# The last convolution on two row halves of PE, kept pieces of x and early loads, in a two-layer image kernel

## The chip, the cores and the metric

The kernel runs on one core of one Trainium2 chip. The metric is device time in microseconds: the median of three runs. Beside it stands one execution under the hardware profiler, from which every duration below comes. The engines are named as in the profile: PE (TensorE, matmuls), PEld (its weight loads), DVE (VectorE), ACT (ScalarE), POOL (GpSimd) and SP (SyncE, which here only issues DMAs).

## What is computed

The input x is float32 of shape 4 x 192 x 128 x 128. Two residual layers follow each other, each on a group-normalised input (32 groups of 6 channels):

```python
x = x + L0_conv(gn(x))     # layer 0
x = x + L1_conv(gn(x))     # layer 1: layer norm, projections, a depthwise convolution, a selective scan, a gate
```

Only layer 0 is touched by the change. Cut to its steps, with `C1 = 48` and `C0 = 16`:

```python
x1 = c1x1(x, conv1_w)                            # 192 -> 48 channels
x_0, x_05, x_1 = x1[:, :16], x1[:, 16:32], x1[:, 32:48]
Fre = frft2d(x_05, 0.5)                          # fractional Fourier transform, both axes
mag, pha = abs(Fre), angle(Fre)
mag_out = c1x1(c3x3(mag * mask1) * mask1 + c1x1(mag * mask2) * mask2)
pha_out = c1x1(pha)
ifrft = abs(frft2d(polar(mag_out, pha_out), -0.5))
fre = rfft2(x_1); mo, po = c1x1(abs(fre)), c1x1(angle(fre))
x_1o = irfft2(polar(mo, po))
x_0o = c1x1(x_0)
return c1x1(concat([x_0o, ifrft, x_1o]), conv2_w)   # 48 -> 192 channels
```

## The kernel before

Layer 0 handles one image after the other. An image of 192 x 16384 values is cut into 16 pieces of 1024 columns (`NPIECE`, `PIECE`); a piece of x is a tile `xt` of 96 partitions x 2 x 1024 values, 768 KB, since the 192 channels stand as two halves of 96 (index `t`). Three generators do the work:

- `analysis(b)` (L247) reads the 16 pieces for the group statistics (`bn`, four `bn_stats` a piece, L192), works out the group's mean and scale in `bn_done` (L196), and reads the 16 pieces again for the first convolution (L278), whose output goes to DRAM as `d1` (48 rows). This convolution already puts the two column halves `q` of a piece on the two column halves of PE: weights `w1r[:, t, half]`, output partitions 0 to 63 and 64 to 127.
- `branches(b)` (L291) does the transforms of the image: `spectrum` forward (matmuls L214 and L224, then `_polar` on DVE, ACT and POOL), the convolutions on magnitude and phase (L244, L348), `_from_polar`, and the inverse transforms (L407, L415, then L437, L445). Its output `dimg` (32 rows) is written to DRAM at L453. It yields 26 times.
- `synthesis(b)` (L456) does the last convolution and the residual. For each piece it loads x once more (L461), loads a tile `cat` of 49 rows (16 rows of `d1`, 32 of `dimg`, one row of ones `orow` for the bias), multiplies it with the folded weights `w2x` (49 x 192, L471), adds the result to `xt` (L475), takes the statistics for layer 1 (L476), and stores the sum to `xmid` with a DMA from POOL (L477).

For each half `q` of 512 columns, a tile `pr` of two PSUM banks takes the two output halves `t`; both matmuls stand on PE's first rows:

```python
pr = psB.tile([128, 2, 512], F32, name="pr")
for t in range(2):
    nc.tensor.matmul(pr[0:CH, t, :], w2x[:, t * CH : (t + 1) * CH], cat[:, at], start=True, stop=True)
nc.vector.tensor_add(xt[:, :, at], xt[:, :, at], pr[0:CH])
```

A float32 matmul runs as two passes, each with its own weight load: the profile counts 512 of them at L471 for 64 pieces x 4 matmuls.

The generators are interleaved by the loop at the end of `layer0` (L489): at each of the 26 steps of `branches(b)`, `analysis(b + 1)` goes one step, and then either `analysis(b + 1)` (odd steps) or `synthesis(b - 1)` (even steps) goes one more. What is left of both is run after the last step. The last image has no `analysis` beside it, so `synthesis(2)` gets its 13 even steps there and three pieces afterwards; `synthesis(3)` follows alone.

The order on the engines is not the program's order word for word: outside of layer 1 (whose order is written by hand) a scheduler puts instructions in the order of its own plan, and inserts the waits. The program's order is its priority. Each engine then runs its list in that order. Loads, `cat` loads and the transfers of the branches all stand in one queue, SP's; a DMA that has to wait for its buffer holds up what is behind it.

Buffers that matter: `xt` has 6 (pool `l0x`), `cat` 2, `pr` 2 (pool `l0r`, shared with `spectrum`), `ps` 4. A piece's `xt` becomes free when its last reader is done, in `synthesis` when its store has landed.

Layer 1 begins when `bn_done` of the last image is through, because its constants `nmr` (L554) need the statistics of all images.

Of the kernel before, what the change touches and what calls it, by code (L numbers as in the profile page):

```python
# [10 lines left out]
F32 = mybir.dt.float32  # L11
# [8 lines left out]
C = 192  # L20
CH = 96
GROUP = 6
NC = 16
# [9 lines left out]
PIECE = ROWS * S  # L33
NPIECE = S // ROWS
# [87 lines left out]
def layer0(tc, x, xmid, st2, w):  # L122

    nc = tc.nc
    B = x.shape[0]
    with ExitStack() as ctx:
        def pool(name, bufs, **kw):
            return ctx.enter_context(tc.tile_pool(name=name, bufs=bufs, **kw))

        cp = pool("l0c", 1)  # L130
        dram = pool("l0d", 2, space=DRAM)
        xp = pool("l0x", 6)
        sp = pool("l0s", 2)
        imp = pool("l0i", 2)
        zp = pool("l0z", 2)
# [1 line left out]
        qp = pool("l0q", 1)  # L137
# [3 lines left out]
        def const(name):  # L141
            src = w[name]
            t = cp.tile(list(src.shape), F32, name="c_" + name)
            nc.sync.dma_start(out=t, in_=src)
            return t
# [3 lines left out]
        ri_cat, ri_out = const("ri_cat"), const("ri_out")  # L149


        w2x = cp.tile([3 * NC + 1, C], F32, name="w2x")
        nc.sync.dma_start(out=w2x[NC : 3 * NC, :], in_=w["w2T"][NC:, :])
        w20, c0 = cp.tile([NC, C], F32, name="w20"), const("c0")
        nc.sync.dma_start(out=w20, in_=w["w2T"][0:NC, :])
        ps = psA.tile([128, 512], F32, name="ps")
        nc.tensor.matmul(ps[0 : NC + 1, 0:C], c0, w20, start=True, stop=True)
        folded = cp.tile([NC + 1, C], F32, name="folded")
        nc.vector.tensor_copy(folded, ps[0 : NC + 1, 0:C])
        nc.sync.dma_start(out=w2x[0:NC, :], in_=folded[0:NC, :])  # L160
        nc.sync.dma_start(out=w2x[3 * NC :, :], in_=folded[NC:, :])
        half_pi = cp.tile([128, 1], F32, name="half_pi")
        nc.vector.memset(half_pi, math.pi / 2)

# [4 lines left out]
        dmag = []  # L169
        zrow = cp.tile([1, S], F32, name="zrow")  # L170
        nc.vector.memset(zrow, 0.0)
        orow = cp.tile([1, PIECE], F32, name="orow")
        nc.vector.memset(orow, 1.0)
        for i in range(min(2, B)):
            d = dram.tile([NC * S + 2, S], F32, name=f"dmag{i}", bufs=1)
            nc.sync.dma_start(out=d[0:1, :], in_=zrow)
# [3 lines left out]
        def split(v):  # L180
            return v.rearrange("(t p) f -> p t f", p=CH)

        def load(b, p):
            xt = xp.tile([CH, 2, PIECE], F32, name="xt")
            src = x[b].rearrange("c h w -> c (h w)")[:, p * PIECE : (p + 1) * PIECE]
            nc.sync.dma_start(out=xt, in_=split(src))
            return xt

        def bn(st, p, xt):
            for t in range(2):  # L190
                for q in range(PIECE // 512):
                    nc.vector.bn_stats(  # L192
                        st[:, t, p * (PIECE // 512) + q, :], xt[:, t, q * 512 : (q + 1) * 512]
                    )

        def bn_done(st, out):  # L196
            mv = sp.tile([CH, 2, 2], F32, name="mv")
            for t in range(2):
                nc.vector.bn_aggr(mv[:, t, :], st[:, t, :, :])
            _group_stats(nc, sp, psA, g_ones, mv, out, 1e-5)  # L200
# [46 lines left out]
        def analysis(b, got):  # L247


            st = sp.tile([CH, 2, NPIECE * (PIECE // 512), 6], F32, name="st")  # L250
            for p in range(NPIECE):
                bn(st, p, load(b, p))
                yield
            gst = sp.tile([CH, 2, 2], F32, name="gst")
            bn_done(st, gst)

            w1r = sp.tile([CH, 2, 128], F32, name="w1r")
            for t in range(2):  # L260
                nc.vector.tensor_scalar(w1r[:, t, :], w1T[:, t, :], gst[:, t, 1:2], None, ALU.mult)
            ps = psA.tile([128, 512], F32, name="ps")
            for t in range(2):
                nc.tensor.matmul(
                    ps[:, 0:1], w1r[:, t, :], gst[:, t, 0:1], start=t == 0, stop=t == 1
                )
            b1 = sp.tile([128, 1], F32, name="b1")
            nc.vector.tensor_scalar(b1, ps[:, 0:1], -1.0, None, ALU.mult)
            d1 = got["d1"] = dram.tile([3 * NC, S * S], F32, name="d1")
            for p in range(NPIECE):  # L270
                xt = load(b, p)
                if p % 2 == 0:
                    x1 = sp.tile([128, 2, 512], F32, name="x1")
                ps = psA.tile([128, 512], F32, name="ps")
                for t in range(2):
                    for q in range(2):
                        half = slice(64 * q, 64 * (q + 1))
                        nc.tensor.matmul(  # L278
                            ps[half], w1r[:, t, half], xt[:, t, q * 512 : (q + 1) * 512],
                            start=t == 0, stop=t == 1,  # L280
                        )
                nc.scalar.activation(x1[:, p % 2, :], ps, AF.Identity, bias=b1)
                if p % 2 == 1:
                    at = d1[:, (p - 1) * PIECE : (p + 1) * PIECE].rearrange(
                        "c (e q f) -> q c e f", e=2, q=2
                    )
                    for q in range(2):
                        nc.scalar.dma_start(out=at[q], in_=x1[64 * q : 64 * q + 3 * NC])
                yield
# [163 lines left out]
            nc.sync.dma_start(out=dimg.rearrange("c h w -> h c w"), in_=img)  # L453
            got.update(dimg=dimg)

        def synthesis(b, got):  # L456

            d1, dimg = got["d1"], got["dimg"].rearrange("c h w -> c (h w)")
            st = sp.tile([CH, 2, NPIECE * (PIECE // 512), 6], F32, name="st2")
            for p in range(NPIECE):  # L460
                xt = load(b, p)  # L461
                cat = qp.tile([3 * NC + 1, PIECE], F32, name="cat", bufs=2)
                at = slice(p * PIECE, (p + 1) * PIECE)
                nc.sync.dma_start(out=cat[0:NC, :], in_=d1[0:NC, at])
                nc.sync.dma_start(out=cat[NC : 3 * NC, :], in_=dimg[:, at])
                nc.sync.dma_start(out=cat[3 * NC :, :], in_=orow)
                for q in range(PIECE // 512):
                    at = slice(q * 512, (q + 1) * 512)
                    pr = psB.tile([128, 2, 512], F32, name="pr")
                    for t in range(2):  # L470
                        nc.tensor.matmul(  # L471
                            pr[0:CH, t, :], w2x[:, t * CH : (t + 1) * CH], cat[:, at],
                            start=True, stop=True,
                        )
                    nc.vector.tensor_add(xt[:, :, at], xt[:, :, at], pr[0:CH])  # L475
                bn(st, p, xt)  # L476
                nc.gpsimd.dma_start(  # L477
                    out=split(xmid[b][:, p * PIECE : (p + 1) * PIECE]), in_=xt
                )
                yield  # L480
            bn_done(st, st2[:, b])

        got = [{} for _ in range(B)]
        for _ in analysis(0, got[0]):
            pass
        behind = iter(())
        for b in range(B):  # L489
            ahead = analysis(b + 1, got[b + 1]) if b + 1 < B else iter(())  # L490
            for i, _ in enumerate(branches(b, got[b])):
                next(ahead, None)
                next(ahead if i % 2 else behind, None)
            for rest in (behind, ahead):
                for _ in rest:
                    pass
            behind = synthesis(b, got[b])
        for _ in behind:
            pass

# [3 lines left out]
def layer1(tc, xmid, out, st2, w, n_tok=S * S):  # L504

    nc = tc.nc
    B = len(xmid)
    NCHUNK = n_tok // T
# [8 lines left out]
    with ExitStack() as ctx:  # L517
# [35 lines left out]

        nmr = cp.tile([CH, B, 2], F32, name="nmr")  # L554
        nc.vector.scalar_tensor_tensor(
# [600 lines left out]
def program(tc, x, out, w):  # L1156
    B = x.shape[0]
    with (
        tc.tile_pool(name="keep", bufs=1) as keep,
        tc.tile_pool(name="mid", bufs=1, space=DRAM) as mid,  # L1160
    ):
        st2 = keep.tile([CH, B, 2, 2], F32, name="st2")
        xmid = [mid.tile([C, S * S], F32, name=f"xmid{b}") for b in range(B)]
        layer0(tc, x, xmid, st2, w)
        layer1(tc, xmid, [out[b].rearrange("c h w -> c (h w)") for b in range(B)], st2, w)
# [16 lines left out]
```

## Time and profile before

| what | us |
|---|---|
| median of 3 runs (lowest, highest) | 11733.97 (11728.79, 11737.78) |
| the profiled execution, whole | 11752.54 |
| its span, first to last instruction | 11750.5 |
| `dimg` of image 0, 1, 2, 3 issued to DRAM | 401.6, 700.8, 1035.8, 1308.5 |
| first matmul of the last `synthesis` | 1326.35 |
| end of its last statistics | 1438.9 |
| median time to landing: `xt` load, `xmid` store, `dimg` write | 9.4, 7.2, 14.8 |

How to read it: busy times are sums over a stretch, so a share of busy time averages over stages with different limits. What ends a wait is named behind an arrow, by engine, tile and line. In the lists of the timeline the columns are start, duration, engine, line, operation, output and inputs, and how many are merged; in brackets, the idle time before and what ended it. "SPq" and "ACTq" are DMAs issued from those engines. The granted clock is that of PE, as a fraction of full speed.

Over the whole span DVE is busy 92%, POOL 86%, PE 85% and ACT 73%, but that is layer 1's picture, which fills seven eighths of the time. Layer 0 has its own, and differs from stage to stage.

### The profile page before, as it was taken

Reading aid. Unit: us, or ns where it says so; the run is one execution under the profiler, and the core shown is the slowest. Engines: PE = TensorE matmul, PEld = TensorE weight load, DVE = VectorE, ACT = ScalarE, POOL = GpSimd, SP = SyncE. Lnnn points to the kernel's source line nnn. Section 1 sums busy time; section 2 is a strip of 40 time slices with the busy share of each in tenths; the row PEclk is TensorE's granted clock in tenths of the full one; section 3 lists DMA queues with packets and bytes.
Section 4 is the critical chain, followed back from the end, with each engine's and each line's share of the span. In section 5 each row is a group of like instructions: output and inputs, shape, how many; then the busy total and the mean of one; then the engine's idle time right before and its main releaser. Section 6 shows DMA issues by size and latency. Waiting matters only on the chain.

```text
span 11750.5 us, 153548 instructions
## 1 busy us (share of the span) xinstructions
PE 9994.0 (85%) x50570; PEld 6788.1 (58%) x50570; DVE 10759.5 (92%) x11584; ACT 8606.6 (73%) x14436; POOL 10087.8 (86%) x4598
## 2 busy tenths in 40 slices
PE   4777888888888888888888888888888888888887
PEld 2444456666666666666666666666666666666665
DVE  5565579999999999999999999999999999999999
ACT  2322178788888788788788788788888878878876
POOL 0000089999999999999999999999999999999999
PEclk8888689999999999999999999999999999999998
DMA  8887633433433443443443443443343343344343
GB/s 208 209 223 194 185 109 113 124 114 111 124 117 108 124 123 103 126 125 100 126 124 102 123 124 106 120 124 108 117 124 113 113 124 115 111 124 118 108 124 97
DMA packets 1339384, 1494.09 MB, mean 127 GB/s; under 512 B 903473, under 2 KB 954358, under 8 KB 1338070
## 3 DMA queue, kind: packets, MB, share of 16 engines
q1 hardware_dynamic: 1318102, 1421.34, 42.0%
q0 software_dynamic: 13312, 50.34, 1.3%
q10 hardware_dynamic: 7168, 12.59, 0.3%
q8 instruction: 398, 6.52, 0.2%
q14 instruction: 404, 3.31, 0.1%
HBM read 1325.19 MB, written 155.32 MB: 126 GB/s over the span
## 4 chain that ended last, share of the span: by engine, by line
DVE 42%; ACT 20%; PE 19%; issue 12%; DMA 4%; POOL 1%; DVEq 1%; SPq 0%; ACTq 0%; POOLq 0%
DVE h L868 29%; DVE op L819 10%; PE py L894 5%; ACT da L799 5%; ACT op L799 4%; PE ps L663 3%; ACT dbT L843 2%; ACT L799 2%; PE pr L471 2%; PE py L908 2%; ACT dt L744 1%; DMA xt<-in_x 1%; ACT L744 1%; DMA bc<-dbc 1%; PE ps L653 1%
## 5 line engine op out<-in xcount | busy, mean ns | idle before, releaser
L881 POOL TENSOR_TENSOR hc<-h,bc 128x1024 f32<-128x1024 f32 x3072 | 7198.0, 2366 | 244.7 <-DVE h L868 218.7
L868 DVE TENSOR_TENSOR_SCAN h<-da,carry,op 128x512 f32<-128x512 f32 x3968 | 4945.7, 1271 | 2.3 <-issue 0.5
L894 PE MATMUL py<-ident,hc 128*128 128x128 f32 x24576 | 3482.6, 291 | 680.1 <-ACT yt L903 653.5
L894 PEld LDWEIGHTS py<-ident,hc 128*128 128x128 f32 x24576 | 3049.8, 151 | 1585.1 <-issue 754.3
L799 ACT ACTIVATE da<-dt,c_A_log 128x512 f32<-128x512 f32 x4096 | 2813.7, 721 | 558.2 <-DVE h L868 551.9
L868 DVE TENSOR_TENSOR_SCAN h<-op,carry,db 128x512 f32<-128x512 f32 x1984 | 2522.3, 1271 | 84.2 <-issue 82.2
L827 POOL TENSOR_TENSOR db<-dtu,bc 128x1024 f32<-128x1024 f32 x1024 | 2419.6, 2363 | 7.9 <-DMA bc<-dbc 7.8
L819 DVE TENSOR_TENSOR op<-dp,bc 128x512 f32<-128x512 f32 x3328 | 2252.5, 677 | 32.9 <-ACT dp L782 32.9
L799 ACT ACTIVATE op<-dt,c_A_log 128x512 f32<-128x512 f32 x2048 | 1398.8, 689 | 979.0 <-DVE h L868 978.8
L663 PE MATMUL ps<-s,c_wiT 96*128 96x512 f32 x3072 | 1468.5, 601 | 38.4 <-DVE s L657 38.4
L681 PE MATMUL ps<-xs,dcw 128*128 128x512 f32 x3072 | 1424.3, 592 | 0.2 <-ACT xs L676 0.2
L799 ACT ACT_TABLE_LOAD x636 | 816.0, 1283 | 11.5 <-DVE h L868 0.3
L843 ACT ACTIVATE dbT<-ps,bT 128x128 f32<-128x128 f32 x3072 | 822.0, 371 | 0.0
L932 PE MATMUL ps<-yg,c_woT 128*96 128x512 f32 x1536 | 711.8, 599 | 112.6 <-DVE xm L938 112.6
L663 PEld LDWEIGHTS ps<-s,c_wiT 96*128 96x128 f32 x3072 | 531.3, 193 | 445.9 <-issue 376.7
L681 PEld LDWEIGHTS ps<-xs,dcw 128*128 128x128 f32 x3072 | 533.1, 190 | 432.5 <-issue 432.1
L477 POOL DMA_DIRECT2D xmid<-xt x64 | 42.9, 671 | 782.6 <-DVE xt L475 775.9
L908 PE MATMUL py<-ddp,u 128*128 128x128 f32 x3072 | 536.0, 333 | 0.0
L633 PE MATMUL ps<-ones,xs 96*128 96x1 f32 x2048 | 346.2, 299 | 199.0 <-ACT dt L744 194.2
L932 PEld LDWEIGHTS ps<-yg,c_woT 128*96 128x96 f32 x1536 | 240.2, 163 | 472.0 <-issue 318.9
L908 PEld LDWEIGHTS py<-ddp,u 128*128 128x128 f32 x3072 | 511.1, 251 | 0.0
L748 POOL TENSOR_TENSOR dtu<-dt,u 128x512 f32<-128x512 f32 x384 | 476.6, 1269 | 30.1 <-ACT dt L744 30.1
(172 smaller groups left out, 10267.7 us busy)
## 6 DMA issues: line engine op xcount, KB each, us to landing
bc<-dbc SPq DMA_DIRECT2D x1024, 1024.0 KB, 5.9
xt<-in_x SPq DMA_DIRECT2D x192, 768.0 KB, 9.4
xmid<-xt POOLq DMA_DIRECT2D x64, 768.0 KB, 7.2
xm<-xmid SPq DMA_DIRECT2D x128, 384.0 KB, 3.6
carry<-h SPq DMA_DIRECT2D x3072, 1.0 KB, 1.9
out<-xm SPq DMA_DIRECT2D x128, 384.0 KB, 3.3
d<-x ACTq DMA_DIRECT2D x64, 192.0 KB, 7.8
df<-u SPq DMA_DIRECT2D x16, 512.0 KB, 4.9
```

The lines of the kernel that those rows point to most:

```text
L663: nc.tensor.matmul(pp, wiT[:, t, m * 128 : (m + 1) * 128], s[:, t, :], start=t == 0, stop=t == 1)
L681: nc.tensor.matmul(pc, dcw[:, j, k, :], xs[:, j, k : k + T], start=k == 0, stop=k == 3)
L748: nc.gpsimd.tensor_tensor(dtu[j], dt[j], u[j], ALU.mult)
L799: nc.scalar.activation(da, got[n]["dt"][j], AF.Exp, scale=A[:, j, st : st + 1])
L819: nc.vector.tensor_tensor(dbs[s], g["dp"], g["bc", k % NG][:, 0, q, :], ALU.mult)
L827: nc.gpsimd.tensor_tensor(db, _bc(g["dtu"][j], 1, G), g["bc", sg][:, 0], ALU.mult)
L843: nc.scalar.activation(t[:, blk, :], g["tu", j][:, blk, :], AF.Identity, scale=g["bT"][:, blk, q : q + 1])
L868: nc.vector.tensor_tensor_scan(h[:, q, :], das.pop(s), dbs.pop(s) if db is None else db[:, q, :], 0.0 if ch == 0 else g["before"][:, j, st ...
L881: nc.gpsimd.tensor_tensor(hc, h, g["bc", sg][:, 1], ALU.mult)
L894: nc.tensor.matmul(py[:, blk, :], hc[:, q, blk * 128 : (blk + 1) * 128], ident, start=first, stop=sg == NG - 1 and q == G - 1 and blk == T ...
L908: nc.tensor.matmul(got[n]["py", j][:, blk, :], got[n]["u"][j][:, blk * 128 : (blk + 1) * 128], ddp[:, j, :], start=False, stop=False, skip ...
L932: nc.tensor.matmul(po[0:CH], woT[:, j, t * CH : (t + 1) * CH], g["yg", j], start=j == 0, stop=j == NJ - 1,)
```

## The change

The second convolution's tile `cat` becomes two fixed tiles of 128 x 512 values instead of a rotating one of 49 x 1024. Half `q` of a piece is loaded into rows 64q to 64q + 47, and row 64q + 48 holds a one that is written once, at the start; `orow` and its load for each piece go. The weights `w2x` are held twice, on rows 0 to 48 and 64 to 112. A `pr` tile now belongs to one output half `t`, and its two matmuls take the two halves `q`, each from its own rows; the addition runs over all 1024 columns of one `t`.

In `analysis`, the last four pieces of the statistics stay on chip (`KEEP`), and the first convolution begins with them; they aren't read a second time. The pool of `xt` has 7 buffers instead of 6.

For the last image, `synthesis(2)` goes a step at every step of `branches(3)`, and at step 18 (`LOADS`) the first four pieces of x for `synthesis(3)` are loaded (`early`).

```diff
-        xp = pool("l0x", 6)
+        xp = pool("l0x", 7)
...
-        w2x = cp.tile([3 * NC + 1, C], F32, name="w2x")
-        nc.sync.dma_start(out=w2x[NC : 3 * NC, :], in_=w["w2T"][NC:, :])
+        w2x = cp.tile([128, C], F32, name="w2x")
+        for q in range(2):
+            nc.sync.dma_start(out=w2x[64 * q + NC : 64 * q + 3 * NC, :], in_=w["w2T"][NC:, :])
...
-        nc.sync.dma_start(out=w2x[0:NC, :], in_=folded[0:NC, :])
-        nc.sync.dma_start(out=w2x[3 * NC :, :], in_=folded[NC:, :])
+        for q in range(2):
+            nc.sync.dma_start(out=w2x[64 * q : 64 * q + NC, :], in_=folded[0:NC, :])
+            nc.sync.dma_start(
+                out=w2x[64 * q + 3 * NC : 64 * q + 3 * NC + 1, :], in_=folded[NC:, :]
+            )
...
-        orow = cp.tile([1, PIECE], F32, name="orow")
-        nc.vector.memset(orow, 1.0)
+        cats = [cp.tile([128, 512], F32, name=f"cat{i}") for i in range(2)]
+        for cat in cats:
+            nc.vector.memset(cat, 1.0)
...
+            kept = {}
             for p in range(NPIECE):
-                bn(st, p, load(b, p))
+                xt = load(b, p)
+                if p >= NPIECE - KEEP:
+                    kept[p] = xt
+                bn(st, p, xt)
                 yield
...
-            for p in range(NPIECE):
-                xt = load(b, p)
+            for p in (*range(NPIECE - KEEP, NPIECE), *range(NPIECE - KEEP)):
+                xt = kept.pop(p, None) or load(b, p)
...
-        def synthesis(b, got):
+        def synthesis(b, got, early):
...
-                xt = load(b, p)
-                cat = qp.tile([3 * NC + 1, PIECE], F32, name="cat", bufs=2)
-                at = slice(p * PIECE, (p + 1) * PIECE)
-                nc.sync.dma_start(out=cat[0:NC, :], in_=d1[0:NC, at])
-                nc.sync.dma_start(out=cat[NC : 3 * NC, :], in_=dimg[:, at])
-                nc.sync.dma_start(out=cat[3 * NC :, :], in_=orow)
-                for q in range(PIECE // 512):
-                    at = slice(q * 512, (q + 1) * 512)
+                xt = early[p] if p < len(early) else load(b, p)
+                cat = cats[p % 2]
+                for q in range(2):
+                    at = slice(p * PIECE + q * 512, p * PIECE + (q + 1) * 512)
+                    nc.sync.dma_start(out=cat[64 * q : 64 * q + NC, :], in_=d1[0:NC, at])
+                    nc.sync.dma_start(out=cat[64 * q + NC : 64 * q + 3 * NC, :], in_=dimg[:, at])
+                for t in range(2):
                     pr = psB.tile([128, 2, 512], F32, name="pr")
-                    for t in range(2):
+                    for q in range(2):
+                        rows = slice(64 * q, 64 * q + 3 * NC + 1)
                         nc.tensor.matmul(
-                            pr[0:CH, t, :], w2x[:, t * CH : (t + 1) * CH], cat[:, at],
+                            pr[0:CH, q, :], w2x[rows, t * CH : (t + 1) * CH], cat[rows, :],
                             start=True, stop=True,
                         )
-                    nc.vector.tensor_add(xt[:, :, at], xt[:, :, at], pr[0:CH])
+                    nc.vector.tensor_add(
+                        xt[:, t, :], xt[:, t, :], pr[0:CH].rearrange("p q f -> p (q f)")
+                    )
...
+            early = []
             for i, _ in enumerate(branches(b, got[b])):
                 next(ahead, None)
-                next(ahead if i % 2 else behind, None)
+                next(ahead if i % 2 and b < B - 1 else behind, None)
+                if b == B - 1 and i == LOADS:
+                    early = [load(b, p) for p in range(KEEP)]
...
-            behind = synthesis(b, got[b])
+            behind = synthesis(b, got[b], early)
```

## The prediction

> **What bounds the kernel now.** The profiled execution spans 11750.5 us (11752.54 us with what lies around it), 18.6 us above the median of the runs, 11733.97. I first cut the span by stage, at the four moments when `dimg` of an image is written out (401.6, 700.8, 1035.8 and 1308.5 us), at the first matmul of the last `synthesis` and at its end. Columns: stretch, length, busy us of PE, PE loads, DVE, ACT, POOL, then granted clock, DMA share, GB/s.
>
> ```profile
> 0.00:140.00 140.00, 42.14 (x138) 13.06 (x138) 53.06 (x92) 12.13 (x18) 0.20 (x4) 0.89 0.95 253
> 402.00:701.00 299.00, 236.23 (x775) 125.38 (x774) 174.91 (x205) 86.43 (x117) 23.29 (x24) 0.83 0.77 204
> 701.00:1036.00 335.00, 254.31 (x830) 134.55 (x829) 207.79 (x262) 89.79 (x123) 23.96 (x27) 0.81 0.84 220
> 1036.00:1309.00 273.00, 222.13 (x707) 126.75 (x706) 176.74 (x201) 76.56 (x104) 25.05 (x29) 0.82 0.62 169
> 1326.30:1440.00 113.70, 109.51 (x128) 35.67 (x128) 79.32 (x98) 0.00 (x0) 10.08 (x16) 0.50 0.74 215
> 1440.00:11750.00 10310.00, 8943.97 (x47260) 6235.84 (x47260) 9907.33 (x10526) 8249.14 (x13946) 9990.52 (x4486) 0.93 0.39 116
> ```
>
> The last row is the second layer, 10310 us, which the change doesn't touch. It starts from the statistics of all four images, so what the first 1440 us lose is gained one for one. In them I see three regimes: a head of 140 us on DMA (share 0.95), three mixed cycles of 273 to 335 us in which no engine is full (PE 76 to 81%, DVE 58 to 65%), and a tail of 113.7 us in which PE is full at half clock. The chain of waits says the same of the tail, in one piece:
>
> ```profile
> 1326.35 109.52 PE pr L471 x128
> ```
>
> The timeline shows one piece of it. PE runs eight passes, two to each of its four matmuls, one every 0.853 us: 6.83 us a piece. Each addition is released by PE:
>
> ```profile
> 1354.59 0.28 PEld L471 LDWEIGHTS pr<-cat,w2x 49*96 49x96 f32 x1 [0.57 <-issue]
> 1355.44 0.28 PEld L471 LDWEIGHTS pr<-cat,w2x 49*96 49x96 f32 x1 [0.57 <-issue]
> ...
> 1357.38 1.22 DVE L475 TENSOR_TENSOR xt<-xt,pr 96x1024 f32<-96x1024 f32 x1 [0.41 <-PE pr L471]
> ...
> 1360.80 1.22 DVE L475 TENSOR_TENSOR xt<-xt,pr 96x1024 f32<-96x1024 f32 x1 [1.47 <-PE pr L471]
> ```
>
> What DVE needs for a piece when nothing holds it up stands in the second cycle: two additions in 2.27 us to the next start, four statistics in 2.46, so 4.73 us.
>
> ```profile
> 925.34 2.35 DVE L475 TENSOR_TENSOR xt<-xt,pr 96x1024 f32<-96x1024 f32 x2 [6.02 <-DMA xt<-in_x]
> 927.61 2.46 DVE L192 BATCH_NORM_STATS2 st<-xt 96x6 f32<-96x512 f32 x4
> ```
>
> And the first convolution, L278, already alternates two halves of PE (columns there). Its weight loads come in twos every 0.43 us at full clock; at half clock (around 78 us) in twos every 0.85.
>
> ```profile
> 80.31 0.14 PEld L278 LDWEIGHTS ps<-xt,w1r 96*64 96x64 f32 x2 [0.29 <-issue]
> ...
> 80.74 0.14 PEld L278 LDWEIGHTS ps<-xt,w1r 96*64 96x64 f32 x2 [0.29 <-issue]
> ```
>
> Last, the waits of DVE in the first 1445 us (total, times, longest): a quarter of these two is DMA.
>
> ```profile
> DVE xt L475 <- PE pr L471: 212.0, 67, 25.5
> DVE xt L475 <- DMA xt<-in_x: 65.6, 6, 25.3
> ```
>
> **What the Trainium skill says.** "TensorEngine Tiling (Array Packing)", Key Properties: different tiles of the array can load weights and multiply in parallel, and its table under Theoretical Speedup gives up to 2x for a dimension of at most 64. The contraction here has 49 rows, and the twos of L278 show such a doubling for column halves; row halves are in no row of this trace. The same page, PSUM Bottleneck: faster tiles don't speed up the reading of PSUM, which may become the limit. Here that is the 4.73 us of DVE. "TensorE: Matmul & The Clock Gate", Part 1: a PE kept busy for some 4 us gets its full clock. The tail disagrees: busy 109.5 of 113.7 us, granted 0.50. So I count half clock in the tail after as well. "Trainium Kernel Development and Optimization", Key Constraints: transfers issued from SP, ACT and POOL share the same 16 DMA engines. That fits the 0.74 share in the tail, where loads and stores run together.
>
> **The change part by part.**
>
> Tail. The two matmuls of a `pr` now stand on rows 0 to 48 and 64 to 112 and write different banks. If they overlap as L278 does, a piece takes four slots of 0.853 us, 3.41 us, below the 4.73 of DVE. So DVE is late next. A `pr` is free again when its addition ends; then PE needs three slots (2.56 us: first pass, two together, last pass) while DVE has the other addition and four statistics, 3.6 us. DVE doesn't wait. New tail: 2.56 + 16 x 4.73 = 78.2 us against 112.5 before (1326.35 to the end of the last statistics, 1438.9), 34 less; 1 us goes to four `cat<-dimg` issues ahead of the first piece where there were two (0.4 us each). **33 us saved.** Could DMA hold it up? A piece costs 0.74 x 6.83 = 5.05 us of all DMA engines now. The order of SP's queue after the change has 9 loads of x behind the last `dimg` write, 7 pieces being on chip or in flight. A load is 2.2 us of that by its bytes and 3.0 by the head; at 2.6 the tail needs 16 x 5.05 - 7 x 2.6 = 63 us of DMA against 78: it fits. The SP queue too: 1.97 us of issuing a piece (xt 0.51, twice 0.31 and 0.42) for 1.74 now. Behind a blocked load stand the next `cat` loads; the load of piece p+7 waits for the store of piece p (7.2 us to land), which is over two pieces before those `cat` are wanted. Ends: 20 (two `cat` loads late by a few us each) to 36.
>
> Head. Image 0 reads 28 pieces of x where it read 32; a piece arrives every 3.2 us (0.95 of DMA): 12.8 us less. It gives some back. At the turn four of seven buffers are held, so three loads run ahead of the convolution where six did; DMA then stands from about 74.5, when the third lands, to about 79, when the first kept piece has been read (the first three passes of L278 run at half clock, 3.4 us a piece). **8 us saved**, between 5 and 12.
>
> The cycles of images 1 to 3. In the chain of waits of each, L471 has 10.9% of 299, 8.7% of 335 and 13.6% of 273 us: 33 + 29 + 37 = 99 us. PE's order in the changed program keeps these groups nearly where they were, so they run in half the time: at most 50 us. Behind PE stand DVE, with its own order, and DMA at 0.62 to 0.84, so I count half: **25 us**. Four loads less in each of three images are 38 us of DMA time, with the gain open: the 65.6 us in which DVE waited for x would shrink, but from the last statistics to the convolution four of seven buffers are held, and synthesis of the image behind must share three. Bounds +20 and -25 us; I take zero. The last image brings two small items, together taken at zero: three pieces of the image behind (3 x 4.73 = 14 us of DVE) move out of the stretch from 1246 to 1313, where L471 stood between the inverse transforms (4.67 us a round with it, 4.45 without), into the 210 us before it, where DVE was busy 165. Cover is 45 us; without it they would cost the 14.
>
> Small ones. `orow` (64 issues of 0.50 us) goes, 128 more `cat` issues come: 12 us more on SP, over 64 pieces, in a queue that mostly waits. Setup: two more weight pieces, under 1 us, beside the constants. Rows of `cat` are 2 KB where they were 4 KB, for 0.2 of 1.77 MB a piece. The additions are the same size.
>
> Sum: 33 + 8 + 25 = 66 us. 11752.5 - 66 = 11686.5 for such an execution; **11668 us** on the scale of the median.
>
> **The rivals.** (B) The cycles give all they show: 50 us of L471 and some 15 of DMA. For it: PE has the longest waits of DVE there. Against: DVE and DMA are close behind. 33 + 8 + 65 = 106 less: 11628. (C) The cycles give nothing, since DVE's and SP's orders hold them where they are: 11734 - 41 = 11693, and with a poor tail 11707. (D) Row halves run one after the other. Nothing in this trace shows them together. Then the tail keeps 6.83 us a piece, and 8 us of the head and a few of the moved pieces remain: 11722, no change that shows. (E) Slower: the held pieces starve the rest. At each of three turns synthesis stands without x, its `cat` and x loads block SP's queue, and the `u<-df` loads behind them, for which PE waits now (31.7 us in all), come late. The price is a wait for x like the longest seen, 25.3 us, and some 5 us more for the late `df`: 30 us a turn, 90 in all, against 66 of gain: 11758. It decides from 22 us a turn.
>
> **How the numbers follow.** Forecast 0.60 (own range 11645 to 11690), B 0.16, C 0.13, D 0.05, E 0.06. The range leaves out the outer half of B, the poorest C, D and E: 11632 to 11707. Runs of this kernel agree within 0.1%, so 0.2% (23.5 us) is what can be told from no change. Faster by more: forecast, B and nearly all of C, 0.87; within: D and the rest of C, 0.07; slower: E, 0.06.
>
> **What would show it.** Right: in the last `synthesis`, weight loads in twos, additions without a wait on PE, 4.7 to 5 us a piece, some 80 us in all; x loads of image 0 end near 111 us instead of 119. Wrong: passes 0.85 us apart one by one (D), additions released by `cat` or x (DMA), or cycles longer than now with waits on `xt<-in_x` above 65.6 us (E).

## The result, and the profile after

The kernel after takes 11671.15 us (median, 11667.05 to 11678.49); the kernel before, on the same chip, 11732.83. The ratio is 0.9948, with a 95% interval of 0.9931 to 0.9965. The forecast was 11668.

The profiled execution of after spans 11672.6 us, 77.9 less than that of before. That is more than the change gave. From the end of the last statistics on, the second layer took 10293.8 us in this profile and 10311.6 in that of before; the change touches nothing there, and every other profile of this study has 10307 to 10314. The first layer is what counts: its last statistics end at 1378.8 us where they ended at 1438.9, 60.1 us earlier. The medians differ by 61.7.

The same stages as shown of before, in the view by stretches (stretch, length, busy us of PE, PE loads, DVE, ACT, POOL, then granted clock, DMA share, GB/s):

```profile
0.00:140.00 140.00, 40.37 (x143) 13.79 (x144) 55.68 (x97) 11.90 (x19) 0.20 (x4) 0.89 0.90 241
390.00:690.00 300.00, 226.04 (x791) 121.17 (x790) 182.09 (x219) 88.00 (x120) 24.03 (x25) 0.82 0.75 202
690.00:1012.50 322.50, 236.34 (x826) 127.94 (x827) 200.72 (x251) 89.87 (x123) 23.65 (x27) 0.80 0.81 214
1012.50:1281.50 269.00, 193.01 (x708) 115.87 (x705) 179.88 (x210) 76.95 (x105) 24.77 (x29) 0.84 0.66 176
1292.06:1378.77 86.71, 67.77 (x128) 21.94 (x128) 75.32 (x97) 0.00 (x0) 10.11 (x16) 0.50 0.85 254
1383.00:11672.00 10289.00, 8943.15 (x47256) 6238.19 (x47256) 9901.39 (x10518) 8248.83 (x13945) 9989.95 (x4485) 0.93 0.39 116
```

PE was full in the tail, 109.5 of 113.7 us. Now it is busy 67.8 of 86.7, still at half clock, and DVE is busy 75.3. The cycles moved less: 402 became 390, 299 stayed 300, 335 became 322.5 and 273 became 269.

The timeline shows the overlap that no row of before could show. Weight loads of the two row halves come in twos and fours, and where nothing holds them the eight passes of a piece take 3.80 us, where before took 6.83 and the prediction had 3.41:

```profile
1300.63 3.80 PE L484 MATMUL pr<-cat,w2x 49*96 49x512 f32 x8 [0.88 <-DVE xt L488]
...
1312.09 0.76 PEld L484 LDWEIGHTS pr<-cat,w2x 49*96 49x96 f32 x4 [4.66 <-issue]
...
1313.06 0.65 PEld L484 LDWEIGHTS pr<-cat,w2x 49*96 49x96 f32 x2 [0.21 <-issue]
...
1313.91 0.65 PEld L484 LDWEIGHTS pr<-cat,w2x 49*96 49x96 f32 x2 [0.20 <-issue]
```

Where nothing else holds them, additions and statistics of DVE stand end to end, one piece every 4.63 us:

```profile
1304.01 2.33 DVE L488 TENSOR_TENSOR xt<-xt,pr 96x1024 f32<-96x1024 f32 x2
...
1306.26 2.46 DVE L201 BATCH_NORM_STATS2 st<-xt 96x6 f32<-96x512 f32 x4
...
1308.64 2.33 DVE L488 TENSOR_TENSOR xt<-xt,pr 96x1024 f32<-96x1024 f32 x2
```

But the chain of waits of this tail is no longer one piece of PE. It alternates between PE and the small loads of `cat` (start, us, what; pieces of it are left out):

```profile
1304.74 7.25 DMA cat<-dimg
...
1316.20 6.28 DMA cat<-dimg
...
1337.84 6.76 DMA cat<-dimg
...
1344.74 17.40 PE pr L484 x27
...
1362.46 7.71 DMA cat<-dimg
```

The waits of DVE in the first 1383 us (total, times, longest) fell where the change meant to make them fall, and one grew from 36.4 to 66.8 us: the wait of L461 (L448 before), the last transforms of an image. It comes back with the experiments on the last image.

```profile
DVE xt L488 <- PE pr L484: 95.1, 24, 23.2
DVE img L461 <- PE ps L458: 66.8, 10, 31.7
DVE xt L488 <- DMA xt<-in_x: 41.6, 5, 19.8
```

### The profile page after: what moved, and what is told of

Read it like the earlier page. It is cut to its first block, busy times and chain, and to the rows that moved or that the text cites. A ratio compares the mean times of both kernels' runs of the same rounds, so it can differ in the third digit from the quotient of the medians.

```text
span 11672.6 us, 153623 instructions
## 1 busy us (share of the span) xinstructions
PE 9888.1 (85%) x50570; PEld 6752.3 (58%) x50570; DVE 10749.9 (92%) x11585; ACT 8606.6 (74%) x14436; POOL 10087.2 (86%) x4598
## 3 DMA queue, kind: packets, MB, share of 16 engines
q1 hardware_dynamic: 1317958, 1408.54, 41.6%
## 4 chain that ended last, share of the span: by engine, by line
DVE 41%; PE 21%; ACT 20%; issue 12%; DMA 4%; POOL 1%; DVEq 0%; SPq 0%; POOLq 0%; ACTq 0%
DVE h L886 28%; DVE op L837 10%; PE py L912 6%; ACT da L817 5%; ACT op L817 4%; PE ps L681 3%; ACT dbT L861 2%; ACT L817 2%; PE py L926 2%; PE ps L651 1%; DMA bc<-dbc 1%; PE ps L699 1%; POOL hc L899 1%; ACT L762 1%; PE op L872 1%
## 5 line engine op out<-in xcount | busy, mean ns | idle before, releaser
L886 DVE TENSOR_TENSOR_SCAN h<-op,carry,db 128x512 f32<-128x512 f32 x1984 | 2508.4, 1264 | 85.3 <-issue 83.2
L837 DVE TENSOR_TENSOR op<-dp,bc 128x512 f32<-128x512 f32 x3328 | 2228.1, 670 | 33.4 <-ACT dp L800 33.4
```

Source lines behind the costliest of these rows:

```text
L837: nc.vector.tensor_tensor(dbs[s], g["dp"], g["bc", k % NG][:, 0, q, :], ALU.mult)
L886: nc.vector.tensor_tensor_scan(h[:, q, :], das.pop(s), dbs.pop(s) if db is None else db[:, q, :], 0.0 if ch == 0 else g["before"][:, j, st ...
```

## The experiments

Twelve runs followed, of eleven further kernels and of after once more. They ran on two other chips, on which the kernel before takes 11753 and 11755 us instead of 11733. So the table gives each median's distance from that of before on the same chip. The other columns are us of one profile: the four cycles (each up to the issue of an image's `dimg` write), the gap from the last write to the first matmul of the last `synthesis`, that `synthesis` up to its last statistics, and the time at which these end.

| kernel | from before (ratio, interval) | cycles 0 to 3 | gap | tail | ends at |
|---|---|---|---|---|---|
| before | 0 | 401.6, 299.2, 335.0, 272.7 | 17.8 | 112.5 | 1438.9 |
| after | -61.7 (0.9948, .9931 to .9965) | 390.2, 299.6, 322.6, 269.1 | 10.5 | 86.7 | 1378.8 |
| after_again | -63.0 (0.9946, .9933 to .9958) | 394.4, 300.9, 320.0, 267.3 | 10.6 | 85.3 | 1378.4 |
| rows_seq | -27.6 (0.9978, .9968 to .9987) | 388.5, 307.9, 323.1, 269.5 | 10.6 | 113.2 | 1412.7 |
| rows_alone | -77.7 (0.9934, .9921 to .9946) | 402.0, 297.1, 324.3, 247.1 | 16.1 | 85.1 | 1371.6 |
| last_off | -71.9 (0.9939, .9927 to .9952) | 390.7, 303.1, 319.5, 250.0 | 16.1 | 85.3 | 1364.7 |
| early_off | -61.8 (0.9945, .9933 to .9958) | 391.7, 301.6, 324.2, 262.7 | 10.5 | 86.9 | 1377.6 |
| keep_off | -70.2 (0.9945, .9933 to .9958) | 397.7, 294.1, 322.2, 263.3 | 10.6 | 85.2 | 1373.0 |
| no_overlap | -66.5 (0.9946, .9933 to .9960) | 392.2, 295.9, 308.6, 276.2 | 11.0 | 92.5 | 1376.4 |
| before_pad | -55.9 (0.9954, .9942 to .9967) | 400.9, 289.3, 327.6, 260.5 | 18.0 | 95.1 | 1391.4 |
| cats4 | -100.1 (0.9919, .9905 to .9932) | 388.2, 298.0, 310.1, 255.8 | 10.6 | 77.4 | 1340.0 |
| best | -102.8 (0.9914, .9901 to .9928) | 393.7, 295.0, 308.1, 250.9 | 10.5 | 77.5 | 1335.7 |
| best_64 | -107.5 (0.9909, .9894 to .9924) | 393.0, 294.8, 311.1, 250.0 | 10.5 | 76.9 | 1336.4 |
| best_full | -118.4 (0.9901, .9887 to .9914) | 394.6, 285.5, 308.4, 241.7 | 11.2 | 78.8 | 1320.2 |

**How far one profile can be trusted: after_again.** The kernel after, unchanged.

> The kernel after, unchanged, beside the three others and the same runs of the kernel before. Theory (the second layer simply took 16 us less on the chip of the first comparison, 10294 us against 10311 in every other profile): the ratio to before stays at 0.9948, so about 61 us less than before, and the first layer ends near 1379 us again. Rival (one profile of the first layer can't be told from another within 10 us): the first layer ends more than 5 us away from 1379.

Its ratio is the same, its first layer ends 0.4 us from the first profile's, and its second layer took 10310.1 us. Single cycles differ by up to 4.2 us between the two, so I read nothing below 5 us out of one cycle of one profile.

**Are the row halves the gain? First try, and a surprise: no_overlap.** Each matmul contracts over rows 0 to 112, with a second copy of the weights that is zero in the other half:

```
-   rows = slice(64 * q, 64 * q + 3 * NC + 1)
+   rows = slice(0, 64 + 3 * NC + 1)
-   pr[0:CH, q, :], w2x[rows, t * CH : (t + 1) * CH], cat[rows, :],
+   pr[0:CH, q, :], w2x[rows, q, t * CH : (t + 1) * CH], cat[rows, :],
```

> The kernel after, with the same loads, tiles and pieces kept, but each matmul of the last convolution contracts over rows 0 to 112 with zero weights in the other half, so two of them can't run side by side. Theory (the row halves carry the tail and most of the gain in the cycles): the last synthesis goes back from 86.7 to about 112 us (16 x 6.83 + what follows), the first three cycles lose 10 to 25 us more, median 11705 to 11720. Rival (kept pieces and early loads carry the cycles, the row halves only the tail): +25 us, about 11696, cycle lengths within 4 us of those after (390.2, 299.6, 322.7, 269.0). Second rival (the overlap gives little even in the tail, the gain there is the early loads): tail under 95 us, median under 11682.

Neither the theory nor its first rival held: the time is that of after, and the tail 92.5 us, not 112. The tail's row says why:

```profile
1283.90:1376.40 92.50, 67.45 (x128) 22.80 (x128) 75.45 (x97) 0.00 (x0) 10.15 (x16) 0.89 0.77 236
```

The granted clock is 0.89, where it was 0.50 in the tails of before and after. Eight passes one after the other at 0.43 us take the 3.4 us of four slots at 0.85. The second rival's signs came (a tail under 95 us, and the time of after), but not for its reason, the early loads: early_off, below, shows that these do nothing. This run took the overlap away and gave a second thing in its place, so it says nothing on the overlap. It needed another control.

**Second try: rows_seq.** The same four loads a piece, but both put on rows 0 to 48, side by side in a [49, 1024] tile. (Room for it came from one buffer each for the two tiles of statistics, and from two setup constants.)

```
-   nc.sync.dma_start(out=cat[64 * q : 64 * q + NC, :], in_=d1[0:NC, at])
+   nc.sync.dma_start(out=cat[0:NC, q * 512 : (q + 1) * 512], in_=d1[0:NC, at])
-   pr[0:CH, q, :], w2x[rows, t * CH : (t + 1) * CH], cat[rows, :],
+   pr[0:CH, q, :], w2x[rows, t * CH : (t + 1) * CH], cat[rows, q * 512 : (q + 1) * 512],
```

> The kernel after with the same four small loads of a piece, but both 512 columns of the piece put on rows 0 to 48, so two matmuls can't run side by side and still contract over 49 rows. Theory (the run with 113 rows kept its time only since its tail was granted 0.87 to 0.93 of the clock instead of 0.50; at 49 rows the clock stays at half): clock in the tail 0.50, passes every 0.85 us, tail 110 to 114 us from 86.7, 25 to 50 us slower than after. Rival (the clock follows whether two row halves are in use or how dense PE is, and rows 0 to 48 alone now get full clock): tail 88 to 95 us, within 10 us of after.

The theory held. Half clock, and the passes again stand apart one by one:

```profile
1299.60:1412.70 113.10, 109.48 (x128) 34.99 (x128) 76.26 (x97) 0.00 (x0) 10.13 (x16) 0.50 0.64 195
```

```profile
1330.37 0.28 PEld L484 LDWEIGHTS pr<-cat,w2x 49*96 49x96 f32 x1 [0.57 <-issue]
1331.23 0.28 PEld L484 LDWEIGHTS pr<-cat,w2x 49*96 49x96 f32 x1 [0.57 <-issue]
```

The instructions of PE and DVE stand in nearly the same order as in after, so little but the overlap differs in this pair. It is worth 35 us by the medians beside each other (11725.5 to 11690.2), 34 by the ends of the first layer. Some 27 of them are in the tail, and only 7 in the three cycles and what precedes them (last `dimg` write at 1289.0, against 1281.5 and 1282.6).

**The row halves without the rest: rows_alone.** Six x buffers, nothing kept, no early loads, the old interleaving:

```
-   KEEP = 4
+   KEEP = 0
-   xp = pool("l0x", 7)
+   xp = pool("l0x", 6)
-   next(ahead if i % 2 and b < B - 1 else behind, None)
+   next(ahead if i % 2 else behind, None)
-   if b == B - 1 and i == LOADS:
-       early = [load(b, p) for p in range(KEEP)]
```

> The kernel before with the row halves alone: six x buffers, nothing kept, no early loads, interleaving as before. Theory (row halves carry the gain, keeping is worth 8 us at the head and costs as much in later cycles, the last image's edits cost 14): first write of dimg near 400, last cycle near 250, tail 85 to 88, ratio to before 0.993 to 0.995, so no slower than after. Rival (the three parts add up as the prediction has them, row halves for 58 us of 66 and 8 for the head): 8 to 12 us slower than after.

The theory held. It is 14.7 us faster than the whole change by the medians (11675.5 to 11690.2, five runs each, no overlap of their ranges), and 7 us by the end of the first layer. So the other parts of the change together cost time. The last cycle shows where: 247.1 us here, 267 to 269 in after.

**The last image: last_off and early_off.** The first undoes both edits of the last image (the last two of the diff above) and keeps the rest, the second undoes only the loads ahead.

> The kernel after, but the last image is interleaved as before and no x loads are issued ahead. Theory (the four early loads no longer compete with the dimg write and its first reads, which is where 7 us between the last dimg write and the first matmul went): dimg write lands in about 14 us where it takes 9.1, the gap from its issue to the first matmul is back at 17 to 18 us from 10.5, the tail a few us longer by four more loads in it; 8 to 14 us slower, 11679 to 11685. Rival (landing is short for another reason, such as fewer x loads behind it in any case): gap stays near 10 to 12 us and the median is within 4 us of 11671.

> The kernel after with its interleaving of the last image, but without x loads issued ahead. Theory (the interleaving, which packs the synthesis of the third image into the first half of the last image's transforms, is what makes the last cycle 269 us where the run without both had 250): last cycle 265 to 273, gap from dimg write to first matmul back at 16 us, first layer ends near 1385, 3 to 8 us slower than after. Rival (the early loads stand in SP's queue ahead of loads that PE waits for, and they make it long): last cycle 248 to 256, first layer ends near 1366, 10 to 15 us faster than after.

I had expected last_off to be slower; it is faster. The loads ahead do nothing that can be seen: without them the median is 11691.3, with them 11690.2. PE and DVE go through the same order in both, and nine loads of x follow the last `dimg` write in both. The rival of early_off, that these loads block SP's queue, falls. The interleaving does two things (early_off against last_off). It shortens the gap from 16.1 to 10.5 us, which I had put down to the loads ahead. And it makes the last cycle 13 us longer, 19 us if after's cycle is taken. Undoing it is worth 14 us by the first layer's end and 6.7 by the medians (11683.5 to 11690.2, on two chips with the kernel before at 11755 and 11753; the ranges just don't overlap). The size is somewhere between these. How it costs is seen when the last cycle is cut where the two halves of the phase, `ph`, are read (L352). First early_off, with the new interleaving:

```profile
1017.50:1121.90 104.40, 74.11 (x288) 46.05 (x286) 91.26 (x103) 34.78 (x47) 13.89 (x13) 0.82 0.73 204
1121.90:1158.00 36.10, 25.71 (x75) 11.83 (x73) 34.95 (x37) 6.99 (x9) 1.26 (x2) 0.86 0.89 192
1158.00:1280.20 122.20, 90.26 (x347) 56.33 (x346) 53.56 (x71) 35.20 (x50) 9.60 (x14) 0.89 0.54 156
```

Then last_off, with the old one:

```profile
1013.20:1108.70 95.50, 64.73 (x253) 42.70 (x251) 75.96 (x83) 33.99 (x46) 12.22 (x10) 0.80 0.64 177
1108.70:1134.50 25.80, 17.95 (x50) 9.02 (x50) 24.78 (x25) 5.49 (x7) 0.63 (x1) 0.80 0.70 149
1134.50:1263.30 128.80, 109.61 (x404) 61.74 (x400) 77.66 (x96) 36.96 (x52) 11.95 (x18) 0.89 0.71 194
```

With the new interleaving the first two stretches are 19 us longer, and DVE is busy 126.2 of their 140.5 us, 34.95 of 36.10 in the second: it has done the additions of 12 of the 16 pieces of `synthesis` by their end, against 8 with the old one. Four pieces at 4.63 us are nearly these 19 us, so DVE has become the bound there. In the third stretch it is busy 53.6 of 122, and only 6.6 us come back. Its idle time is the wait that grew in after (15.0 us in last_off):

```profile
DVE img L461 <- PE ps L458: 48.6, 4, 31.7
```

**The kept pieces: keep_off.** All 32 loads of x for the analysis of every image, as before; the four loads ahead of the last image stay.

```
-   KEEP = 4
+   KEEP = 0
```

> The kernel after, but no piece is kept from the statistics to the first convolution: all 32 loads of x for an image's analysis are issued, the loads ahead of the last image stay. Theory (keeping is worth its loads only at the head, where DMA is full): 8 to 12 us slower, about 11681, all of it before the first dimg write (390 becomes about 400). Rival (fewer loads also make the cycles shorter, above all the third, which lost 12 us): +25 to +35 us, 11696 to 11706, third cycle back to about 335 from 322.7. Second rival (held buffers starve the cycles): the cycles shrink by 5 to 10 us and the total stays at 11671 or falls.

Neither the theory nor the first rival held; the second rival is nearest. Keeping gains at the head (cycle 0 is 390 to 394 with it, 398 without), and seems to lose some 5 us each in cycles 1 and 3 (300 to 301 with it, 294 without; 267 to 269 with it, 263 without), which is at the edge of what one cycle can show: early_off keeps its pieces and has 262.7 in cycle 3. Over all it can't be told from nothing: 11685.2 without (11682.0 to 11698.3), 11690.2 with (11685.8 to 11694.1, on the other chip).

**What holds the tail: cats4.** Four `cat` tiles for two, with the room found as in rows_seq:

```
-   cats = [cp.tile([128, 512], F32, name=f"cat{i}") for i in range(2)]
+   cats = [cp.tile([128, 512], F32, name=f"cat{i}") for i in range(4)]
-   cat = cats[p % 2]
+   cat = cats[p % 4]
```

> The kernel after with four cat tiles in place of two (room from one buffer each for the two tiles of statistics). Theory (in the tail, two cat tiles let the four small loads of a piece start only when PE has left the tile, and their 5.5 us landing then holds PE: some 8 us of the tail): waits of PE on cat loads in the last synthesis nearly vanish, tail 78 to 80 us from 86.7, 6 to 9 us faster, about 11663. Rival (the tail is held by DMA throughput, 0.85 of all engines busy at 254 GB/s): the wait moves to x loads, tail 84 to 87 us, median 11668 to 11673.

For the tail the theory held, and it is the 78.2 us of the prediction's sum less 0.8. The whole gain is far more than the 6 to 9 us expected: 37 us by the distances from before, 38 to 39 by the end of the first layer. In this stretch DVE is busy 74.4 of 77.3 us:

```profile
1262.70:1340.00 77.30, 61.84 (x128) 17.92 (x128) 74.39 (x97) 0.00 (x0) 10.15 (x16) 0.50 0.88 284
```

and of PE's waits for `cat` (22.7 us, 7 times, in after) only the first, which is the gap, is left:

```profile
PE pr L484 <- DMA cat<-dimg: 11.4, 1, 11.4
```

DMA throughput was not the limit: 284 GB/s move here where 254 moved. The loads of `cat` land even later than in after (6.3 us in the median against 5.4), but they are issued two pieces earlier. The rest of the gain, 10 to 13 us each in cycles 2 and 3, I had not expected. Having one buffer each for the tiles of statistics doesn't bring it, since rows_seq has that too and the cycles of after. The scheduler also gave PE and DVE another order than in after, so the run doesn't say whether the buffers or the order shortened the cycles.

**Together: best.** Row halves, four `cat` tiles, the old interleaving, no loads ahead, and pieces kept for image 0 alone (`if b == 0 and p >= NPIECE - KEEP`).

> The row halves with four cat tiles, the last image interleaved as before, no early loads, and pieces kept for image 0 alone. Theory (the parts add up: 8 to 10 us at the head, DVE no longer crowded in the last cycle, no wait on cat in the tail): cycles about 390, 295, 310 to 320, 240 to 250, gap 16, tail 77 to 79, first layer ends at 1330 to 1340, ratio to before 0.990 to 0.9915, at or below the run with four cat tiles alone (0.9919). Rival (four cat tiles already took what the old interleaving gives, since they too shortened the last cycle, to 256): no better than 0.9919, first layer ends at 1340 to 1350.

Between the two: it ends at 1335.7 us, but the median is only 3 us below that of cats4, with ranges that overlap. Four `cat` tiles had already taken most of what the old interleaving gives. The gap is not the 16 us expected but 10.5, although the old interleaving is back.

**The clock: before_pad, best_64, best_full.** The first pads the kernel before and changes nothing else in it:

```
-   w2x = cp.tile([3 * NC + 1, C], F32, name="w2x")
+   w2x = cp.tile([113, C], F32, name="w2x")
+   nc.vector.memset(w2x, 0.0)
...
-   cat = qp.tile([3 * NC + 1, PIECE], F32, name="cat", bufs=2)
+   cat = cats[p % 2]
```

Its `cats` are two fixed tiles of 113 rows, set to ones at the start. best_64 and best_full are made from best, "the first of these" in what was expected of them; "the same" means best too.

> The kernel before with its 49 rows of the last convolution padded to 113 (rows 49 to 112 of cat hold ones, their weights are zero). Nothing else differs: same loads, eight passes a piece one after the other. Theory (the half clock of the tail comes with the 49 rows): tail at 0.85 to 0.95 of the clock, passes 0.43 us apart, 78 to 92 us from 112.5, 20 to 45 us faster than before. Rival (it needs real data in both halves, or the clock in the tail follows something else): clock 0.50, tail 110 to 114, time within 5 us of before.

> The first of these, with each row half contracting over 64 rows (15 of them with zero weights) where it took 49. Theory (the granted clock follows the rows that a matmul contracts over, with a point between 49 and 113): if that point lies below 64, the tail is granted 0.85 or more, still with two row halves at once, and the cycles get up to 10 us shorter; if above, clock 0.50 and the time of the first within 5 us. The tail's length says nothing here, since DVE sets it.

> The same with each matmul of the last convolution over rows 0 to 112 and zero weights in the other half, so nothing overlaps but the tail should be granted about 0.9 of the clock. Theory (with cat there in time, eight passes of 0.43 us, 3.45 us a piece, are below the 4.63 of DVE as the overlapped four of 0.85 are): tail 77 to 82 us, cycles within 10 us of the overlapped version, medians within 10 us of each other. Rival (the passes of the overlapped version are cheaper where PE shares its time with the transforms): 10 to 25 us slower, all in the cycles.

Padding alone makes the kernel before 56 us faster by the medians and 48 by the end of the first layer, eight to nine tenths of what the whole change brought, without an overlap. That is more than the 20 to 45 expected. Its tail is granted 0.84; passes are 0.43 us apart except at its start, where they were still 0.85. At 95.1 us it is 17 us shorter, though 3 above the range expected.

```profile
1296.00:1391.40 95.40, 70.62 (x128) 23.29 (x128) 76.32 (x97) 0.00 (x0) 10.11 (x16) 0.84 0.85 253
```

The tails of best, best_64 and best_full, in this order, differ in PE and its clock and not in their length, since DVE sets it (74.3 to 74.5 us busy):

```profile
1258.20:1335.70 77.50, 59.78 (x128) 17.05 (x128) 74.43 (x97) 0.00 (x0) 10.07 (x16) 0.54 0.87 283
```

```profile
1259.40:1336.40 77.00, 50.15 (x128) 13.58 (x128) 74.34 (x97) 0.00 (x0) 10.11 (x16) 0.72 0.88 285
```

```profile
1241.40:1320.20 78.80, 61.01 (x128) 20.33 (x128) 74.50 (x97) 0.00 (x0) 10.07 (x16) 0.95 0.84 275
```

The mixed cycles gain too. PE and DVE of before_pad stand in nearly the same order as in before; its cycles 1 to 3 were granted 0.87, 0.85 and 0.89 where before had 0.83, 0.81 and 0.82, and are 10, 7 and 12 us shorter. best_full was granted 0.90, 0.87 and 0.89, best 0.84, 0.83 and 0.84, and best_full wrote its last `dimg` 17.5 us earlier; here the order differs as well, so that this is the clock alone isn't shown. best_full is the fastest of all, 118 us below before, where after is 63 below. Each of its cycles is within 10 us of best's, as its theory had it, but they add up, and the medians are 15.5 apart; its rival had the wrong sign. best_64 falls between its two cases: a clock of 0.72, cycles unchanged, and a median 4.7 us lower.

## Why the prediction was right, and where only its sum was

**The tail: mechanism right, size off.** That the row halves overlap "as L278 does" is shown by after against rows_seq. The clock stayed at half, as assumed. The sum gave 78.2 us and a saving of 33; measured are 86.7 and 85.3, a saving of 26 to 27, inside the ends of 20 and 36. (A piece takes DVE 4.63 us and not 4.73, 1.6 us in 16 pieces the other way.) The term that was mis-sized is the wait for `cat`. I had put "two `cat` loads late by a few us each" into the lower end and nothing into the value. Once PE takes half as long, a tile that comes free starts its loads later relative to the next need: landing took 6.3 to 7.7 us on the chain (2.9 in the median of before's tail), a piece 4.63. cats4, with two more tiles, has no such wait left and lands on the 78. The Trainium skill, "TensorEngine Tiling (Array Packing)", PSUM Bottleneck, warns that the reading of PSUM may become the next limit. In cats4 DVE is that limit, though only its additions read PSUM, 2.25 of its 4.63 us a piece; the statistics read `xt`. In after a loader with two buffers stood before it.

**The head: right.** The first convolution's last passes, which wait for the last x load of image 0, began at 112.9 and 110.6 us instead of 119.3 (expected: loads end near 111). Cycle 0 became 7 to 11 us shorter, 3 to 8 of it by the kept pieces, against a forecast of 8.

**The cycles: the sum near, the parts not.** Cycles 1 to 3 are 15.6 and 18.7 us shorter in the two profiles of after, for a forecast of 25 from the row halves with all else at zero. The row halves with their `cat` tiles, and nothing else, bring 38 (rows_alone: 2, 11 and 26). The step that failed is the last image. The prediction moved three pieces of the image behind "into the 210 us before it, where DVE was busy 165", and counted 45 us of cover: "without it they would cost the 14". The mean over 210 us hid where the cover was. Cut like early_off and last_off, the last cycle of before begins:

```profile
1035.80:1152.40 116.60, 82.19 (x257) 49.27 (x256) 78.94 (x87) 34.04 (x46) 12.39 (x11) 0.74 0.57 160
1152.40:1178.60 26.20, 21.10 (x54) 10.52 (x53) 26.17 (x28) 5.40 (x7) 1.07 (x2) 0.84 0.72 151
```

DVE's idle time was nearly all in the first of these stretches (38 us); in the second it was already full. And a step of `synthesis` at every step of the last image moves more than the three pieces at its end: 12 are done by the end of these stretches in early_off, 8 and a half in before. The cost was 13 to 19 us in that cycle.

**The gap: not in the prediction.** It is 7 us shorter in after. The new interleaving alone brings most of that (early_off 10.5, last_off 16.1), but best has 10.5 with the old one. What the short gaps share is that the image behind is through when `dimg` is written. In before, the last `dimg` write took 15.2 us to land and the first matmul came 2.6 later; in last_off 11.8 and 4.3; in after 8.6 and 1.9; in best 8.7 and 1.8. In the first two, pieces of the image behind are still on DVE during the gap (8.8 and 3.1 us busy) and DMA is 0.83 and 0.91 busy; in after and best DVE has next to nothing to do there and DMA is at 0.75 and 0.76. That this traffic makes the write late is argued from these figures; no run took it away alone.

So the forecast had too much in the tail (6 to 7 us) and in the cycles (6 to 9), and 7 too little in the gap: 60 came of 66. Part of its nearness is luck: errors that met.

**What stays open.** Cycle 2 is 11 to 15 us shorter than before in after, rows_alone and rows_seq alike, though the last has no overlap and the second no kept pieces. So the 11 us of rows_alone's cycle 2 can't be put down to the overlap. The three share the four loads of a `cat`, without `orow`, and additions that take one output half; no run changed these alone. Nor was the overlap taken away under the old interleaving, so how much of the 26 us of rows_alone's last cycle it brings isn't shown.

**The rivals.** D (halves one after the other) is excluded by rows_seq. E (held pieces starve the rest by 22 us a turn) is excluded by keep_off: at most some 7 us a cycle, and DVE's waits of additions for x fell from 65.6 us to 41.6. B had the cycles at 65 us; they gave 16 to 19, and 38 in rows_alone. C had them at nothing, which is further off than the forecast's 25. But for the overlap alone, under the new interleaving, rows_seq shows 7 us, and there C is nearer.

## What to carry to other kernels

When a matmul is made faster, look at once at how its operands arrive: here loads of 6 to 8 us behind two buffers held a loop of 4.6 us, and two more buffers, 4 KB a partition, were worth more (37 us, with the order that the scheduler then chose) than any of the scheduling edits. Cover has to be read at the place to which the work is moved, not as a mean over the stage around it. And test each part of a change alone: one part brought more than the whole, and a control that takes an effect away must be looked at for what it brings in.

## What the runs showed of the hardware

In this kernel the granted clock went with the rows that a matmul contracts over. Tails with 49 rows were granted 0.50 (before and rows_seq one at a time, after and cats4 two halves at once) to 0.54 (best, after_again); two halves of 64 rows, 0.72; 113 rows, 0.84 to 0.95. That includes before_pad, where 64 of the rows have zero weights and which otherwise differs from before only in its fixed `cat` tiles. These are means over a tail: at the start of the padded tails passes still stand 0.85 us apart. How busy PE was doesn't order them: 109.5 of 113.1 us at 0.50, 61.0 of 78.8 at 0.95. The Trainium skill, "TensorE: Matmul & The Clock Gate", Part 1, lets the clock depend on how busy PE has been, and at 49 rows this case disagrees. What of a row's activity counts (its weights' rows, the data streamed over them, the outputs) the runs don't separate.
